# A four-layer graph network on one core: the mixes of layers 1 and 2 as three single passes, and layer 1 written in source order

## The chip, the cores and the metric

The kernel runs on one core of a Trainium2 chip. The metric is the device time of one execution in microseconds (us). The time given is the median of three runs; the profile is of one more execution, whose span and clock are given with it.

## What is computed

`x` has 32 items of 512 nodes with 128 features, in float32. `adj` is a symmetric-patterned 512 x 512 matrix, about an eighth of it nonzero. Four layers follow each other, each on `h = relu(layernorm(x))` with a residual:

```python
# layer 0: softmax over the entries of adj; own node by W[0], the others by W[1]
out = einsum('ij,bjg->big', A * M, h0) + einsum('ij,bjg->big', A * (1.0 - M), h1) + bias
# layer 1: Chebyshev hops with adj (given twice), then one projection
x1 = einsum('bnf,nw->bwf', x0, A);  x2 = 2.0 * einsum('bnf,nw->bwf', x1, A) - x0
out = relu(stack([X, x1, x2, x1, x2]) @ Theta1 + bias)
# layer 2: messages with weights = adj * adj
features = relu(h @ psi_w + psi_b)
messages = einsum('nm,bnd->bmd', weights, features)
out = relu(concat(messages, h) @ phi1_w + phi1_b) @ phi2_w + phi2_b
# layer 3: attention with a mask by adj
A = exp(8 * tanh((x @ q) @ (x @ k).T / sqrt(128) / 8)) * adj
out = (A / sum(A)) @ x @ v
```

Multiplying by the 512 x 512 matrix is called a mix here. Layer 1 has two mixes: the first makes `x1`, and since the second hop is linear, the kernel folds the five blocks of `Theta1` into three matrices `th` and mixes `h th[1] + x1 th[2]` once more, then adds `h th[0]`. Layer 2 has one mix, that of the features.

## The kernel before

The 32 items are taken as 16 pairs `q`; two pairs make a quad `r`, with `A = 2r` and `C = 2r + 1`. The 512 nodes are four tiles of 128 rows. Each item's `x` stays in SBUF from layer to layer; a transposed copy `hT` of the normalized `h` is made by stream transposes on DVE, a store of each quarter to DRAM (`d_hT`) and one load back, all issued by SP.

The mixes of layers 0, 1 and 2 are products of half blocks in the manner of Winograd: seven products of 256 x 256 blocks in place of eight, in float32. `sum_steps` (line 306) makes the sums of blocks of the matrix once, on POOL. `right_blocks` and `right_steps` (lines 343 and 350) make four differences of the right-hand side for each mix (`rt_h`, `rt_feat`, `rt_w`, line 361), on POOL and DVE. `products` (line 370) issues the seven products in the order of `ORDER`, each followed by its eviction:

```python
    ORDER = ((1, "a", True), (6, "c", True), (5, "d", True), (7, "c", False), (2, "a", False),
             (4, "c", False), (3, "d", False))
```

`by_feature` (line 381, matmul at 384) forms them for `x1T` and `msgT`, which come out transposed; `by_token` (line 387, matmul at 391) forms them for layer 0 and for the second mix of layer 1. `mixed` (line 398) evicts with two copies on ACT and six additions on DVE (lines 405 to 424); the evictions of layer 1's second mix are in `layer1` (line 964).

Layer 1 of one quad: normalize and transpose both pairs; `first` (line 978) mixes `h` into `x1T`; `straight` (line 734) copies `hT` into the order of nodes on POOL (`hs`); `weighed` (line 984) projects into `p_w` and copies that to `w` (line 987); the second mix then takes `w`, with the quad's own term `hs` by `th[0]` in the same banks. `layer2` (line 1082) projects features (`feat`, lines 1092 and 1093), mixes them into `msgT`, and applies the two phi projections.

`layer3` (line 1118) already takes its products in parts. A float32 operand is split into a high part, a low part and a middle one, each of type fp32r, and three products of the parts replace one in plain float32:

```python
    def moving_parts(x, high, low, mid):
        nc.scalar.activation(high, x, AF.Copy, scale=DOWN)
        nc.gpsimd.tensor_sub(low, x, high.bitcast(F32))
        nc.vector.scalar_tensor_tensor(mid, x, 1.0 / UP, high.bitcast(F32), OP.mult, OP.subtract)
```

These are lines 434 to 438; `scaled_parts` (line 440) does the same for the query. The scores (line 1155) go through tanh, exp (line 1160) and the mask (line 1162, on DVE and POOL in turn) into `ex`, and line 1172 multiplies `ex` with the values `hv`.

The order of the work: layer 0 stands under a manual schedule, so its instructions on PE, DVE, ACT and POOL run as the source has them. From layer 1 on the scheduler of the language orders instructions by its own estimates. What it is given is a list of generators, one for each quad of layer 1 and each pair of layers 2 and 3; the loop at line 1214 takes a new one in each turn and advances all active ones by one step, so that the steps of neighbouring quads, pairs and layers lie side by side. Buffers are rings of fixed length under a tag: `square` with four (the matrices and `ex`), `quad` with two (`w`, `msgT`, then query and values), `rt` with six, `hs` with six (also features and two parts of the keys), `u` with three (also the third part of the keys), `hT` with four. A new tile of a tag waits until the tile it replaces was last read.

Of the kernel before, what the change touches and what calls it, by code (L numbers as in the profile page):

```python
# [9 lines left out]
F32 = mybir.dt.float32  # L10
# [19 lines left out]
def kernel(  # L30
# [48 lines left out]
    work = ctx.enter_context(tc.tile_pool(name="work", bufs=4))  # L79
    bounce = ctx.enter_context(tc.tile_pool(name="bounce", bufs=4, space=bass.MemoryType.DRAM))  # L80
# [11 lines left out]
    def square_tile(name):  # L92
        return const.tile([P, NT, N], F32, tag="square", name=name, bufs=4)
# [13 lines left out]
    adj_s = square_tile("adj_s")  # L107
# [18 lines left out]
    def load_rows(ap, name):  # L126
        o = ap.shape[0] // P
        w = const.tile([P, o, ap.shape[1]], F32, name=name)
        nc.sync.dma_start(w, ap.rearrange("(o f) g -> f o g", f=P))
        return w  # L130

    def load_bcast(ap, name):
        w = const.tile([P, D], F32, name=name)
        nc.sync.dma_start(w, bass.AP(tensor=ap.tensor, offset=ap.offset, ap=[[0, P], [1, D]]))
        return w
# [6 lines left out]
    qw = load_rows(q_w, "qw")[:, 0, :]  # L142
    kw = load_rows(k_w, "kw")[:, 0, :]
# [6 lines left out]
    w0 = const.tile([P, 2, D], F32, name="w0")  # L150
    nc.sync.dma_start(w0, w_l0.rearrange("o f g -> f o g"))
    b0 = load_bcast(bias_l0, "b0")
# [27 lines left out]
    ident = const.tile([P, P], F32, name="ident")  # L180
# [6 lines left out]
    ones = const.tile([P, P], F32, name="ones")  # L187
# [118 lines left out]
    def sum_steps(mat, name, eng=nc.gpsimd):  # L306

        a11, a12 = mat[:, 0:2, 0:H], mat[:, 2:4, 0:H]
        a21, a22 = mat[:, 0:2, H:N], mat[:, 2:4, H:N]
        extra = const.tile([P, 3, 2, H], F32, tag="sums", name=f"sums_{name}", bufs=2)  # L310
        s1, s2, s4 = extra[:, 0], extra[:, 1], extra[:, 2]
        sums[name] = {1: a11, 2: a12, 3: s4, 4: a22, 5: s1, 6: s2, 7: a21}
        for out, op, p, q in ((s1, OP.add, a21, a22), (s2, OP.subtract, s1, a11),
                              (a21, OP.subtract, a11, a21), (s4, OP.subtract, a12, s2)):
            tc.keep_in_program_order(eng.tensor_tensor(out, p, q, op))
            yield

# [5 lines left out]
    def att_sums():  # L323
# [3 lines left out]
        extra = const.tile([P, 3, 2, H], F32, tag="sums", name="sums_att", bufs=2)  # L327
# [15 lines left out]
    def right_blocks(half, name, engs):  # L343

        right = {}
        for _ in right_steps(half, name, engs, right):
            pass
        return right

    def right_steps(half, name, engs, right):  # L350
        b11, b12, b21, b22 = half(0, 0), half(0, 1), half(1, 0), half(1, 1)
        if len(b11.shape) == 4:
            t = [work.tile([P, 2, 2, D], F32, tag="rt", name=f"rt_{name}_{i}", bufs=6) for i in range(4)]
        else:
            t = []
            for i in range(2):
                two = work.tile([P, 2, 2, D], F32, tag="rt", name=f"rt_{name}_{i}", bufs=6)
                t += [two[:, 0], two[:, 1]]
        right.update({1: b11, 2: b21, 3: b22, 4: t[3], 5: t[0], 6: t[1], 7: t[2]})
        for i, (p, q) in enumerate(((b12, b11), (b22, t[0]), (b22, b12), (b21, t[1]))):  # L360
            engs[i].tensor_sub(t[i], p, q)  # L361
            yield
# [18 lines left out]
    def by_feature(p, a, b, first):  # L381

        for k in range(2):
            nc.tensor.matmul(p[:, :H], b[:, k, :], a[:, k, :], start=(first and k == 0),  # L384
                             stop=(k == 1), skip_group_check=True)

# [8 lines left out]
    def u_tile(name):  # L395
        return work.tile([P, 2, H], F32, tag="u", name=f"u_{name}", bufs=3)

    def mixed(name, left, right, dst):

        m1 = dst[:, 0, H:], dst[:, 1, :H], dst[:, 1, H:]  # L400

        def evict(k, p):
            p = p[:, :H]
            if k == 1:
                nc.scalar.copy(m1[0], p)
            elif k == 6:
                nc.vector.tensor_add(m1[1], p, m1[0])
            elif k == 7:
                nc.vector.tensor_add(m1[2], p, m1[0])
            elif k == 5:  # L410
                return
            elif k == 2:
                nc.scalar.copy(dst[:, 0, :H], p)
            elif k == 4:
                nc.vector.tensor_add(dst[:, 0, H:], p, m1[0])
            elif k == 3:
                nc.vector.tensor_add(dst[:, 1, :H], p, m1[1])

        def evict2(k, p):
            evict(k, p)  # L420
            if k == 5:
                held.append(p)
            if k == 7:
                nc.vector.tensor_add(dst[:, 1, H:], held[0][:, :H], m1[2])

        held = []
        return products(name, by_feature, left, right, evict2)
# [40 lines left out]
    def quad_tile(name):  # L468
        return work.tile([P, 2, 2 * N + 2 * NT], F32, tag="quad", name=name, bufs=2)
# [8 lines left out]
    def project_steps(q, hT, copy=nc.scalar.copy):  # L478
        r, w = divmod(q, 2)
        if w == 0:  # L480
            if r % 3 == 2:
                g[r] = square_tile(f"g_{r}").rearrange("p t (b w f) -> p t b w f", b=2, w=2)
            else:
                t = quad_tile(f"g_{r}").rearrange("p w e -> p (w e)")[:, : 4 * N]
# [243 lines left out]
    late = ctx.enter_context(tc.tile_pool(name="late", bufs=4))  # L728
    for _ in range(NQ // 4, NQ // 2 - 1):
        x_tile(late, NQ // 4 - 1)  # L730
# [3 lines left out]
    def straight(hT, b, scale, name):  # L734

        s = late.tile([P, N], F32, tag="hs", name=name, bufs=6)
        src = hT[:, :, b, :].rearrange("p b (a c) -> p a b c", c=QR)
        if scale is None:
            nc.gpsimd.tensor_copy(split(s), src)
        else:  # L740
            nc.gpsimd.tensor_mul(split(s), src, split(scale))
        return s
# [7 lines left out]
    def late_sums():  # L750

        yield from sum_steps(adj_s, "adj")


        for out, op, p, q in ((1, OP.add, 1, 3), (2, OP.add, 2, 4), (0, OP.subtract, 0, 2)):
            tc.keep_in_program_order(nc.gpsimd.tensor_tensor(th[:, out, :], th[:, p, :], th[:, q, :], op))
            yield
        tc.keep_in_program_order(nc.gpsimd.tensor_scalar(th[:, 2, :], th[:, 2, :], 2.0, None, OP.mult))
# [4 lines left out]
    sums_ahead = late_sums()  # L763
# [36 lines left out]
    def round0(r):  # L800
# [4 lines left out]
        if r == 0:  # L805

            adiag.append(work.tile([P, N], F32, tag="rt", name="adiag", bufs=6))
# [148 lines left out]
    def layer0_stats():  # L956

        yield
        go(own[NQ - 2])
        go(own[NQ - 1])  # L960

    x1 = []

    def layer1(r):

        A, C = 2 * r, 2 * r + 1
        h, hT, right, hs = {}, {}, {}, {}

        def turned(q):
            hT[q] = transposed(h[q], f"hT1_{q}")  # L970
            right[q] = right_blocks(lambda J, b: h[q][:, b, 2 * J : 2 * J + 2, :], f"h_{q}", [nc.gpsimd] * 4)

        def x1T(q):
            if not x1:
                x1.append(square_tile("x1T").rearrange("p (w b) e -> p w b e", w=2))
            return x1[0][:, q % 2]

        def first(q):
            for _ in mixed(f"x1T_{q}", sums["adj"], right[q], x1T(q)):
                pass  # L980
            for b in range(2):
                hs[q, b] = straight(hT[q], b, None, f"hs_{q}_{b}")

        def weighed(q):
            for b in range(2):
                p = projected(f"p_w_{q}_{b}", (columns(hs[q, b]), th[:, 1, :]), (columns(x1T(q)[:, b]), th[:, 2, :]))
                nc.scalar.copy(w1[:, :, b, q % 2, :], p)  # L987

        h[A] = normed(A)
        yield  # L990
        turned(A)
        h[C] = normed(C)
        yield
        first(A)
        turned(C)
        yield
        w1 = quad_tile(f"w_{r}").rearrange("p w e -> p (w e)")[:, : 4 * N]
        w1 = w1.rearrange("p (t b w f) -> p t b w f", t=NT, b=2, w=2)
        weighed(A)
        first(C)  # L1000
        yield

        def operands():
            weighed(C)
            return right_blocks(lambda J, b: w1[:, 2 * J : 2 * J + 2, b], f"w_{r}",
                                [nc.vector] + [nc.gpsimd] * 3)

        sooner = r == 0 or C == NQ - 1
        if sooner:
            right2 = operands()  # L1010
        yield
        if not sooner:
            right2 = operands()
        u = [u_tile(f"l1_{r}_{i}") for i in range(3)]
        held = {}

        def own(p, I, b, first):
            straight_block(p, lambda w: hs[A + w, b], I, th[:, 0, :], first)

        def each(y):  # L1020
            return y.rearrange("p w (i f) -> p w i f", i=2)

        def finish(y, I, b):
            x = x_block(r, I, b).rearrange("p w i f -> p w (i f)")
            nc.vector.scalar_tensor_tensor(x, y, 0.0, x, OP.max, OP.add)

        def done(p, y, I, b):
# [224 lines left out]
```

## Time and profile before

| what | value |
|---|---|
| time, median of 3 runs (lowest to highest) | 946.99 us (946.71 to 947.05) |
| profiled execution, span | 946.18 us, 944.4 us |
| granted TensorE clock | 1.000 of full speed |
| busy: PE, DVE, ACT, POOL | 98%, 73%, 53%, 58% |
| layer 0, about | 0 to 184 us |
| layer 1, about | 184 to 475 us |
| layer 2, about | 446 to 678 us |
| layer 3, about | 678 to 944 us |

The profile counts an engine as busy from the start of its first to the end of its last overlapping instruction. Matmuls are pipelined, so the durations of neighbouring matmuls overlap: 1.03 us for a group of four whose next group starts 0.87 us later. A plain float32 matmul appears as two records, an fp32r one as a single record. "x4" behind a line of the timeline says how many records it stands for. A label such as `p_x1T_a<-adj_s,h` names the output and the inputs by the program's names.

### The profile page before, as it was taken

How to read it: one execution, taken by the hardware profiler on the slowest of the kernel's cores; microseconds unless marked ns; L12 is line 12 of the kernel's file. 1: busy time of each engine (PE TensorE's matmuls, PEld its weight loads, DVE VectorE, ACT ScalarE, POOL GpSimd, SP SyncE). 2: the span in 40 equal slices, each digit the busy share in tenths (PEclk: the TensorE clock that was granted, in tenths of full speed). 3: DMA queues.
4: the chain of work that ended last, by engine and by line, in shares of the span. 5: the costliest groups of instructions: out<-in, count | busy, mean ns of one | idle time of the engine just before them, and what ended most of it. 6: DMA issues, size and time to landing. Idle time of an engine off the chain costs nothing. (4 is left out here: it accounts for less than half of the span.)

```text
span 944.4 us, 15678 instructions
## 1 busy us (share of the span) xinstructions
PE 929.0 (98%) x5625; PEld 811.2 (86%) x5625; DVE 685.4 (73%) x1390; ACT 499.1 (53%) x1120; POOL 543.8 (58%) x536
## 2 busy tenths in 40 slices
PE   8999999999999999999999999999989999999997
PEld 4899999899999999899977787778779899999996
DVE  8888885745555545556667766565699999999995
ACT  5864451451241242365734855545677666666663
POOL 5878997933428524421624334433467878787873
PEclk9999999999999999999999999999999999999999
DMA  9256533242341311424333342223223121212111
GB/s 260 58 157 193 166 112 90 72 131 67 87 122 60 90 32 59 134 67 112 90 112 86 93 128 77 86 68 90 67 60 98 57 79 57 79 57 78 34 35 44
DMA packets 83916, 86.08 MB, mean 91 GB/s; under 512 B 6784, under 2 KB 74624, under 8 KB 83840
## 3 DMA queue, kind: packets, MB, share of 16 engines
q1 hardware_dynamic: 83552, 84.57, 31.8%
q8 instruction: 44, 0.72, 0.3%
q10 hardware_dynamic: 288, 0.52, 0.1%
q14 instruction: 32, 0.26, 0.1%
HBM read 44.17 MB, written 40.89 MB: 90 GB/s over the span
## 5 line engine op out<-in xcount | busy, mean ns | idle before, releaser
L252 ACT ACTIVATE h<-x,sh,rs 128x128 f32<-128x128 f32 x512 | 209.5, 485 | 46.6 <-PE p_x1T_d L384 21.6
L1172 PE MATMUL p_av<-qkh_hv,ex 128*128 128x129 f32 x1024 | 121.8, 276 | 3.2 <-POOL ex L1162 2.2
L1172 PEld LDWEIGHTS p_av<-qkh_hv,ex 128*128 128x128 f32 x1024 | 119.1, 191 | 6.2 <-POOL ex L1162 3.0
L1162 POOL TENSOR_TENSOR ex<-ex,adjTx 128x512 f32<-128x512 f32 x62 | 105.0, 1713 | 6.7 <-issue 5.7
L1162 DVE TENSOR_TENSOR ex<-ex,adjTx 128x512 f32<-128x512 f32 x66 | 87.5, 1331 | 18.4 <-ACT ex L1160 18.4
L288 DVE STREAM_TRANSPOSE hb_hT<-h 128x512 f32<-128x512 f32 x120 | 82.0, 697 | 24.2 <-ACT h L252 23.9
L232 DVE BATCH_NORM_STATS2 bn<-x 128x6 f32<-128x256 f32 x248 | 89.5, 417 | 0.5
L361 POOL TENSOR_TENSOR rt_w<-w,rt_w 128x512 f32<-128x512 f32 x16 | 20.4, 1273 | 110.3 <-DVE rt_w L361 92.0
L361 POOL TENSOR_TENSOR rt_feat<-feat,feat 128x256 f32<-128x256 f32 x16 | 11.6, 725 | 119.4 <-ACT feat L1093 119.4
L1156 ACT ACTIVATE ex<-p_score 128x512 f32<-128x512 f32 x128 | 69.7, 591 | 17.7 <-PE p_score L1155 17.6
L987 ACT COPY w<-p_w 128x512 f32<-128x512 f32 x32 | 18.2, 574 | 106.1 <-PE p_w L464 106.1
L1160 ACT ACTIVATE ex<-ex 128x512 f32<-128x512 f32 x128 | 73.2, 638 | 0.8
L437 POOL TENSOR_TENSOR key_low<-hT,key_high 128x512 fp32r<-128x512 f32 x32 | 54.5, 1702 | 32.2 <-ACT key_high L436 29.7
L444 POOL TENSOR_TENSOR query_mid<-query_high,query_low 128x512 fp32r<-128x512 f32 x32 | 41.2, 1288 | 41.5 <-PE p_qkh L1139 22.2
L442 ACT ACTIVATE query_high<-qkh_hv 128x512 fp32r<-128x512 f32 x32 | 20.2, 633 | 65.0 <-DVE qkh_hv L1142 64.2
L1155 PE MATMUL p_score<-query_high,key_high 128*128 128x512 f32 x128 | 52.4, 417 | 1.9 <-ACT query_high L442 1.9
L1155 PE MATMUL p_score<-query_mid,key_mid 128*128 128x512 f32 x128 | 50.2, 396 | 0.8 <-POOL query_mid L444 0.8
L464 PE MATMUL p_w<-th,hs 128*128 128x128 f32 x256 | 49.5, 275 | 0.0
L464 PE MATMUL p_w<-th,x1T 128*128 128x128 f32 x256 | 49.5, 275 | 0.0
L1155 PE MATMUL p_score<-query_low,key_low 128*128 128x512 f32 x128 | 49.4, 390 | 0.0
L1104 POOL TENSOR_TENSOR x<-x,phi2b 128x256 f32<-128x256 f32 x64 | 45.0, 732 | 0.0
L1093 ACT ACTIVATE feat<-feat 128x512 f32<-128x512 f32 x32 | 20.1, 629 | 41.1 <-DVE feat L1092 41.1
(256 smaller groups left out, 2373.1 us busy)
## 6 DMA issues: line engine op xcount, KB each, us to landing
d_hT<-hb_hT SPq DMA_DIRECT2D x240, 128.0 KB
hT<-d_hT SPq DMA_DIRECT2D x60, 512.0 KB
x<-in_x_dram SPq DMA_DIRECT2D x32, 256.0 KB
out_dram<-x SPq DMA_DIRECT2D x31, 256.0 KB
adjT_d<-adj_squares SPq DMA_DIRECT2D x4, 256.0 KB
sq<-in_adj_dram SPq DMA_DIRECT2D x4, 256.0 KB
adjTx<-adjT_d SPq DMA_DIRECT2D x4, 256.0 KB
adj_s<-in_adj_dram ACTq DMA_DIRECT2D x2, 256.0 KB
```

Source lines behind the costliest of these rows:

```text
L232: nc.vector.bn_stats(st[:, k].rearrange("p e s -> p (e s)"), xt[q][:, b, t : t + 2, :].rearrange("p t f -> p f t"))
L252: nc.scalar.activation(h[:, b, t, :], xt[q][:, b, t, :], AF.Relu, bias=shift[q][:, i : i + 1], scale=scale[q][:, i : i + 1])
L288: nc.vector.transpose(hb[:, :, b].rearrange("p j t r -> p t j r"), h[:, b].rearrange("p t (j c) -> p t j c", c=QR))
L437: nc.gpsimd.tensor_sub(low, x, high.bitcast(F32))
L444: nc.gpsimd.tensor_sub(mid, high.bitcast(F32), low.bitcast(F32))
L464: nc.tensor.matmul(p[:, blk(t)], hT(t), w, start=(i == 0), stop=(i == len(terms) - 1))
L1104: tc.keep_in_program_order(nc.gpsimd.tensor_add(xi, xi, spread(phi2b, 2)))
L1155: nc.tensor.matmul(ps, keys[b][i][:, t, :], query[i], start=(i == 0), stop=(i == 2))
L1156: nc.scalar.activation(ex[:, t, :], ps, AF.Tanh, scale=UP / (8.0 * math.sqrt(D)))
L1160: nc.scalar.activation(ex[:, t, :], ex[:, t, :], AF.Exp, scale=8.0)
L1162: eng.tensor_mul(split(ex[:, t, :]), split(ex[:, t, :]), crossed(adjTx[0][:, t, :]))
L1172: nc.tensor.matmul(po[:, i, : D + 1], ex[:, t, blk(i0 + i)], hv[:, t, :], start=(t == 0), stop=(t == NT - 1))
```

## The change

- `mixed_parts` takes the place of `mixed`: the right-hand side of a mix is split by `moving_parts` into high, low and mid, the matrix was split before, and 3 x 4 matmuls of 128 x 512 in fp32r go into one bank for each item; one ACT copy with a scale evicts it. `x1T` and `msgT` use it. The second mix of layer 1 does the same with the parts of `w`, which `weighed` makes straight from PSUM; its bank also takes the own term, and two DVE operations evict it into `x`. The Winograd form stays for layer 0.
- The block sums of adj and of adj squared go. `late_parts` splits adj into parts during layer 0, on ACT and POOL; `square` splits adj squared during layer 1, on POOL.
- Layer 1 is one generator under the manual schedule for PE, DVE, ACT and POOL. In each quad the second mix of the quad before stands behind the first product of this quad's pair A; the next quad's first product closes it. Two first steps of layer 2 (`more`) are written into the last quad. From there on the scheduler orders the work as before.
- The buffers move: what only layer 0 needs goes into `region0`, which is closed when layer 0 is done, and its room becomes `after`, with `wide_tile` (6 of 128 x 4 x 512: parts of `w`, of the squared matrix, `msgT`, keys, `ex`, values) and `small_tile` (13 of 128 x 512: parts of `h` and of features, `x1T`, features, the query). `matrix_tile` has three: adj, later its three parts, later the transposed mask. `hs` shares the four buffers of `hT`. The mask is loaded at the end of layer 2 instead of in layer 1.

| instructions | before | after |
|---|---|---|
| float32 records of 256 columns, layers 1 and 2 | 1344 | 0 |
| fp32r matmuls of 512 columns, layers 1 and 2 | 0 | 1152 |
| DVE, whole program | 1386 | 1314 |
| ACT | 1120 | 1192 |
| POOL | 541 | 466 |
| SP | 398 | 398 |

The core of the diff (the removal of `sum_steps`, `right_blocks`, `by_feature`, `mixed` and of the old `layer1`, and the moves of small tiles into other pools, are left out):

```diff
+    def matrix_tile(name, dtype=F32):
+        return const.tile([P, NT, N], dtype, tag="matrix", name=name, bufs=3)
+
+    def wide_tile(name, dtype=F32):
+        return after.tile([P, 4, N], dtype, tag="wide", name=name, bufs=6)
+
+    def small_tile(name, dtype=F32):
+        return after.tile([P, N], dtype, tag="small", name=name, bufs=13)
...
+    def mixed_parts(name, left, right, dst):
+
+        p = bank(f"p_{name}")
+        for part in range(3):
+            for t in range(NT):
+                nc.tensor.matmul(p, right[part][:, blk(t)], left[part][:, t, :],
+                                 start=(t == 0 and part == 0), stop=(t == NT - 1 and part == 2))
+        nc.scalar.activation(dst, p, AF.Copy, scale=UP)
...
+    def late_parts():
+
+        adj_parts.extend(matrix_tile(f"adj_{part}", F32R) for part in PARTS[:2])
+        high, low = adj_parts
+        for t in range(NT):
+            nc.scalar.activation(high[:, t, :], adj_s[:, t, :], AF.Copy, scale=DOWN)
+            tc.keep_in_program_order(nc.gpsimd.tensor_sub(adj_s[:, t, :], adj_s[:, t, :], high[:, t, :].bitcast(F32)))
+            yield
...
+        def weighed(q, b):
+            r, j = q // 2, 2 * (q % 2) + b
+            if j == 0:
+                w[r] = [wide_tile(f"w_{part}_{r}", F32R) for part in PARTS]
+            p = projected(f"p_w_{q}_{b}", (columns(hs[q][:, b]), th[:, 1, :]), (columns(x1[q, b]), th[:, 2, :]))
+            high, low, mid = (part.rearrange("p t (w f) -> p t w f", f=D)[:, :, j, :] for part in w[r])
+            nc.scalar.activation(high, p, AF.Copy, scale=DOWN)
+            nc.vector.tensor_sub(low, p, high.bitcast(F32))
+            nc.vector.scalar_tensor_tensor(mid, p, 1.0 / UP, high.bitcast(F32), OP.mult, OP.subtract)
+
+        def mix(r, i):
+            p = bank(f"p_l1_{r}_{i}")
+            for j in range(4):
+                nc.tensor.matmul(p[:, blk(j)], columns(hs[2 * r + j // 2][:, j % 2])(i), th[:, 0, :],
+                                 start=(j == 0), stop=False, skip_group_check=True)
+            for part in range(3):
+                for t in range(NT):
+                    nc.tensor.matmul(p, adj_parts[part][:, t, blk(i)], w[r][part][:, t, :],
+                                     start=False, stop=(part == 2 and t == NT - 1), skip_group_check=True)
+            nc.vector.scalar_tensor_tensor(tiles(p), tiles(p), UP, spread(b1, 4), OP.mult, OP.add)
+            x = xq[r].rearrange("p w b t f -> p (w b) t f")[:, :, i, :]
+            nc.vector.scalar_tensor_tensor(x, tiles(p), 0.0, x, OP.max, OP.add)
...
+        for r in range(NQ // 2):
...
+            else:
+                split_up(A, 1)
+                straighten(A)
+                mix(r - 1, 0)
+                normalised(C, NT)
+                turn(C, 1)
+                mix(r - 1, 1)
+                normalised(C)
+                turn(C)
+                mix(r - 1, 2)
+                split_up(C, 0)
+                go(square, r > 3)
+                mix(r - 1, 3)
+                split_up(C, 1)
+                first(A, 1)
+            weighed(A, 0)
+            weighed(A, 1)
+            go(square, r > 2)
+            first(C, 0)
+            normalised(A + 2, NT)
+            if last:
+                more(0)
+            for q in (A - 2, C - 2) if r else (NQ - 2, NQ - 1):
+                ln_stats(q) if r else go(own[q])
+            first(C, 1)
+            if r:
+                straighten(C)
+            split_up(A + 2, 0)
+            normalised(A + 2)
+            go(square, r > 3)
+            weighed(C, 0)
+            weighed(C, 1)
+            go(square, r > 3)
+            turn(A + 2)
+            first(A + 2, 0)
...
+        more(1)
+        for i in range(NT):
+            mix(r, i)
+            more(2 + i)
+        yield
...
         def key_parts(b):
-            keys[b] = [late.tile([P, NQR, P], F32R, tag="hs", name=f"key_{part}_{q}_{b}", bufs=6) for part in PARTS[:2]]
-            keys[b].append(work.tile([P, NQR, P], F32R, tag="u", name=f"key_{PARTS[2]}_{q}_{b}", bufs=3))
+            both = wide_tile(f"key_{q}_{b}", F32R)
+            keys[b] = [both[:, i].rearrange("p (t n) -> p t n", t=NQR) for i in range(3)]
             moving_parts(hT[:, :, b, :], *keys[b])
...
-            ex = square_tile(f"ex_{q}_{b}")
+            ex = wide_tile(f"ex_{q}_{b}")
```

## The prediction, made before the changed kernel ran

> **What bounds the kernel now.** First the busy shares on the page, to see which engine could set the time:
>
> ```profile
> PE 929.0 (98%) x5625; PEld 811.2 (86%) x5625; DVE 685.4 (73%) x1390; ACT 499.1 (53%) x1120; POOL 543.8 (58%) x536
> ```
>
> PE leads by 27 points. But matmul ends are modelled, so I check what PE waits for (us in total, times, longest):
>
> ```profile
> PE p_av L1172 <- POOL ex L1162: 2.2, 3, 1.0
> PE p_idle L529 <- DVE upto L194: 2.0, 1, 2.0
> PE p_score L1155 <- ACT query_high L442: 1.9, 2, 1.1
> PE p_incl L547 <- DVE rch L542: 1.0, 1, 1.0
> ```
>
> These head the list; all of it is some 15 us, no wait over 2.2. Then the windows by stage (columns: sum, then PE, PEld, DVE, ACT, POOL, clock, DMA share, GB/s): layer 0, 1, their overlap with 2, 2, 3.
>
> ```profile
> 0.00:184.00 184.00, 178.92 (x1116) 157.80 (x1117) 148.45 (x347) 98.07 (x241) 147.63 (x156) 1.00 0.50 138
> 184.00:446.00 262.00, 261.12 (x1544) 237.41 (x1543) 147.13 (x306) 96.89 (x244) 103.20 (x122) 1.00 0.32 90
> 446.00:475.00 29.00, 29.00 (x182) 26.79 (x181) 18.63 (x31) 20.88 (x52) 15.33 (x20) 1.00 0.30 74
> 475.00:678.00 203.00, 202.46 (x1024) 154.70 (x1024) 132.87 (x282) 106.20 (x248) 84.23 (x117) 1.00 0.32 91
> 678.00:944.00 266.00, 257.46 (x1766) 234.46 (x1764) 238.31 (x425) 177.07 (x337) 193.38 (x122) 1.00 0.20 62
> ```
>
> In layers 1 and 2 PE is full and no other engine passes 66%; only layer 3 has DVE near PE (90%). The clock is 1.00 throughout. What a matmul costs is read from starts in the timeline, since the durations overlap. The old mix, then the three-pass scores of layer 3, already in the form the mixes get:
>
> ```profile
> 183.55 1.03 PE L384 MATMUL p_x1T_a<-adj_s,h 128*128 128x256 f32 x4
> 184.42 1.03 PE L384 MATMUL p_x1T_c<-sums_adj,rt_h 128*128 128x256 f32 x4
> 185.28 1.03 PE L384 MATMUL p_x1T_d<-sums_adj,rt_h 128*128 128x256 f32 x4
> ```
>
> ```profile
> 802.69 0.48 PE L1155 MATMUL p_score<-query_high,key_high 128*128 128x512 f32 x1
> 803.01 0.39 PE L1155 MATMUL p_score<-query_low,key_low 128*128 128x512 f32 x1
> ...
> 805.28 0.40 PE L1155 MATMUL p_score<-query_mid,key_mid 128*128 128x512 f32 x1
> ```
>
> Four 256-column f32 records take 0.865 us: 0.216 each. Ten 512-column passes take 2.27: 0.227 each. The first pass after f32 work takes 0.32 instead: a change of form costs about 0.09.
>
> **The skill.** "FP8 and Floating Point Precision", section TensorE Precision Notes: true FP32 is four passes through the array, the reduced form one. The trace agrees: a plain 512-column f32 product shows two records of 0.430, together 3.8 times 0.227. "TensorE: Matmul & The Clock Gate", section Back-to-back issue gap: 512 columns need N/2.4 + 2.5 = 216 ns when isolated; the trace's 227 is used instead. "SBUF — State Buffer", section SBUF: two separate sides: a DVE operation with two SBUF inputs and a GpSimd operation block each other entirely; the trace agrees (query_low on DVE: 0.69 alone, up to 1.78 beside POOL).
>
> **PE, layer 1.** Per quad (four items) the two Winograd mixes have 56 + 56 records: 112 x 0.2165 = 24.2. The quad's own term is 32 records of 128 columns x 0.112 = 3.6, the p_w projection 64 x 0.112 = 7.2: 35.0. After: 48 + 48 passes x 0.228 = 21.9, six changes of form 0.5, the other two unchanged: 33.2. Saved 1.8 x 8 quads = 14.4.
>
> **PE, layer 2.** Per pair 28 x 0.2165 = 6.06 becomes 24 x 0.228 + 0.09 = 5.56; 0.50 x 16 = 8.0. Gain on PE 22.4. Bounds: 16.6 if each of the 64 changes of form costs twice 0.09, 36.2 if the 1152 passes ran at the page's 0.216. I take 22.4, since 0.227 is this trace's own rate for the same form.
>
> **The other engines' work.** Removed: 12 x 16 DVE additions of 0.42 that finish the old mixes; POOL's right-hand differences (64 rt_h and 64 rt_feat of 0.73, 24 rt_w of 1.27); the block sums. Added per 512 columns: high on ACT (0.63), low on POOL (1.27 to 1.70), mid on DVE (0.68 to 1.76) for h and features; for w, high on ACT (0.58 from PSUM) and two on DVE (0.69 each). Two PSUM evictions become one ACT copy of 0.58. Layer 1 per quad after: DVE about 24, ACT 14, POOL 10 of 33 us; layer 2 per pair DVE 8.8, ACT 9, POOL 6 of 12.6. None becomes the bound; what counts is order. In layer 0, splitting adj (8 ACT and 8 POOL steps, 5 and 10 us over five rounds, less the dropped sums) lies in POOL's idle time before its right-hand differences: 0, bounds -1 to +2.
>
> **Waits added in layer 1.** It is now written in source order on PE, DVE, ACT and POOL, so each waits for its next instruction even when a later one is ready. From the order of instructions on each engine in the changed kernel:
> - Per quad: on ACT the copy of x1T(C,1) stands behind four norms and the `sd` of two pairs. Count from W, the first projection of A. DVE finishes the last w parts at W + 2 x 1.79 + 0.8 + 2 x 0.69 = W + 5.8; then eight bn_stats of 0.42, and for the first pair `sd` on ACT, reciprocal and shift, about 2.3: the second `sd` is done at W + 11.4, and the copy ends at about W + 12.0. PE does three projections (5.4), two x1T products (2.8 each) and the hs half of the next step (0.2) first: it wants x1T(C,1) at W + 11.2. Behind the copy stand the w parts of C, hence the next mix. 0.8 x 6 quads = 4.8; bounds 0 and 12, as `sh` on DVE takes 0.16 to 1.0. In the last quad eight norms of layer 2 stand there too: 2.5.
> - Start: high of h(0,1) stands on ACT behind x1T(0,0)'s copy, which waits for PE itself: copy and splits 2.0. hs of pair 1 waits for turn(1), issued late; four stores of 0.45, landing 3.5 and the read 4.6 make 10 us, of which 2.3 shows. The late adj load on SP, ahead of d_hT1_8: 1. From quad 2 the read for A stands on SP behind a store of C; it is a quad (33 us) early: 0.
> Together 12.6, against 2.5 lost there now (261.9 elapsed for 259.4 of work at the rates above): +10.1, bounds +2 and +20.
>
> **Border of layers 1 and 2.** PE goes from the last mix to feat0 and msgT0 in turn. feat0's addition on DVE is behind mix evictions and statistics, then ACT relu and the three parts: about 5.05 after feat0 against 1.8 of PE work: 3.4 idle; the next such place 2.5; 1 elsewhere. 7 against 3.8 now (PE's 202.9 elapsed for 199.1 of work): +3.2, bounds 0 and +8. Today the scheduler interleaves the last quad with layer 2.
>
> **Layer 3.** Same arithmetic. But keys, ex and values share six wide buffers; now the keys have three places of their own, ex three and the values two. So the first tanh of ex(q,0) waits until the last score product has read the keys it replaces, and key_high for two pairs on waits for the scores of a pair before. Behind that tanh stand exp, mask (1.33 on DVE, 1.71 on POOL) and p_av. Margins before p_av are now 0.3 to 1.3 us. Bounds -2 (scheduler luck) and +16; I take +1.5.
>
> Sum: -22.4 + 10.1 + 3.2 + 1.5 = -7.6 on the 944.4 span. The profiled run took 946.18, 0.8 below the median 946.99 of the three timed ones; 946.99 - 7.6 = 939.4.
>
> **Rivals.**
> - *The forecast, a third of the gain kept*: 934 to 944. Chance 0.46.
> - *The waits are absorbed*: PE runs ahead, x1T(C,1) is in time, the border costs 1. For it: 0.8 is a small miss, and PE waits were short everywhere before. Against: four engines in order have no slack to reorder. -22.4 with 3 to 6 lost: 927.6 to 930.6. Chance 0.20.
> - *Passes gain nothing*: changes of form at the upper price leave 16.6, and waits of 15 to 19 take it: 945 to 949. Against: the score rows. Chance 0.10.
> - *Slower: layer 3's wide buffers.* DVE is at 90% there. If the late tanh eats the margin, p_av waits. It decides from 0.35 us a half step on: 32 x 0.35 = 11.2, 9.7 beyond my 1.5, puts the time at 949; at 0.75 it is 962. For it: the longest waits of today are on L1162 and L442, in this chain. Against: a whole half step of 8 us lies between reuse. With layer 1's waits at their upper bound it comes out the same. Chance 0.24.
>
> **Numbers.** Time 939.4. Range 928 to 954: leaves out the upper half of the slower rival (0.12) and the end of the absorbed case (0.04). About 1.9 us (0.2%) is what a measurement here can tell from none. Faster: 0.46, 0.20 and a little of the third: 0.69. Same 0.07, slower 0.24.
>
> **What would show it.** Starts of the passes in the mixes 0.227 apart; layer 1 per quad near 33 us plus under 1.5 of idle; in PE's waits, p_w behind x1T's copy, and p_msgT behind the parts of the first features; p_av's waits little changed. Wrong if layer 3 lasts over 270 us, if a pass in the mixes takes over 0.235, or if PE's waits in layer 1 stay under 3 us or pass 20.

## The result, and the profile after

The changed kernel takes 935.75 us (median of 4 runs, 934.17 to 939.78) against 946.85 us before (946.45 to 947.05): a ratio of 0.989, 95% interval 0.9859 to 0.9921, so 11 us or 1.1% less. The profiled execution, the fastest of the four, has a span of 932.1 us (944.4 before).

The busy line of the changed kernel, then its windows by stage (layer 0, layer 1, layer 2, layer 3; columns as before):

```profile
PE 908.0 (97%) x5433; PEld 777.9 (83%) x5433; DVE 693.7 (74%) x1318; ACT 547.6 (59%) x1192; POOL 530.3 (57%) x461
```

```profile
183.40:457.20 273.80, 268.61 (x1541) 230.75 (x1540) 163.41 (x294) 115.39 (x267) 87.11 (x84) 1.00 0.25 69
457.20:671.00 213.80, 208.19 (x1056) 159.66 (x1056) 143.29 (x262) 161.55 (x357) 105.58 (x102) 0.99 0.42 122
671.00:932.10 261.10, 251.94 (x1732) 230.22 (x1730) 240.91 (x423) 171.13 (x329) 189.29 (x123) 0.99 0.20 61
```

PE is still the engine nearest to full, and it is busy for 21 us less. But its busy time is now 5 us short of the window in layer 1 and 6 in layer 2, where it filled them before, and the clock is 0.99 in two stages. What PE waits for (us in total, times, longest) says where:

```profile
PE p_msgT L383 <- ACT high_feat L397: 4.5, 2, 2.5
PE p_av L1148 <- DVE ex L1138: 3.7, 3, 1.5
PE p_w L425 <- ACT x1T L385: 3.2, 8, 1.7
...
PE p_x1T L383 <- ACT high_h L397: 1.3, 1, 1.3
```

Of the two waits of `p_msgT`, one is at the border of layers 1 and 2 (pair 0), the other at pair 2, some 28 us later. `p_w` waits in every quad for the copy of x1T(C,1), as the prediction said: by start-to-start distances it loses 0.36 us there rather than 0.8, and 1.9 in the last quad.

Steady state, from the start of one quad's projections (one pair's second phi projection, one pair's `p_av`) to the next:

| us | before | after |
|---|---|---|
| quad of layer 1 | 35.06 | 33.65 |
| pair of layer 2 | 13.28 | 12.48 |
| pair of layer 3 | 15.88 | 15.82 |

Eight quads and sixteen pairs at these rates make 11.3 + 12.8 = 24.1 us. From the first product of layer 1 to the last of layer 2 the trace has 500.5 us before and 487.6 after, 12.9 less. So 11 of the 24 us were given back at the edges: 2.0 at the start of layer 1, 1.5 more in its last quad, 2.9 at the border, and 4.8 around the wait of pair 2 in layer 2, of which some 1.7 is not a wait at all (see the filled waits below). The first three are idle times or start-to-start distances of the changed kernel's trace, so this split is rougher than its total. Layer 3 lasts as long as before, 257.4 us for 257.0 from the last product of layer 2 to the last `p_av`.

### The profile page after: what moved, and what is told of

Same layout as the page of the kernel before. It is cut to its first block, busy times and chain, and to the rows that moved or that the text cites. A ratio compares the mean times of both kernels' runs of the same rounds, so it can differ in the third digit from the quotient of the medians.

```text
span 932.1 us, 15187 instructions
## 1 busy us (share of the span) xinstructions
PE 908.0 (97%) x5433; PEld 777.9 (83%) x5433; DVE 693.7 (74%) x1318; ACT 547.6 (59%) x1192; POOL 530.3 (57%) x461
## 4 chain that ended last, share of the span: by engine, by line
PE 87%; ACT 5%; DVE 4%; POOL 2%; issue 1%; DMA 0%; POOLq 0%; ACTq 0%; DVEq 0%
PE p_av L1148 11%; PE p_l L981 10%; PE p_msgT L383 9%; PE p_score L1131 8%; PE p_x1T L383 7%; PE p_w L425 5%; PE p_l_c L371 4%; PE p_l L977 3%; PE p_l_a L371 3%; PE p_l_d L371 3%; PE p_phi L1086 3%; PE p_phi L1087 3%; PE p_g L425 3%; PE p_l L425 3%; PE p_hv L425 3%; PE p_feat L425 3%
## 5 line engine op out<-in xcount | busy, mean ns | idle before, releaser
L1148 PE MATMUL p_av<-hv,ex 128*128 128x129 f32 x1024 | 122.7, 277 | 4.8 <-DVE ex L1138 3.7
L1148 PEld LDWEIGHTS p_av<-hv,ex 128*128 128x128 f32 x1024 | 120.3, 193 | 7.6 <-DVE ex L1138 4.5
L398 POOL TENSOR_TENSOR low_feat<-feat,high_feat 128x512 fp32r<-128x512 f32 x32 | 52.3, 1650 | 119.5 <-ACT high_feat L397 111.5
L398 POOL TENSOR_TENSOR low_h<-h,high_h 128x512 fp32r<-128x512 f32 x32 | 48.5, 1523 | 78.6 <-ACT high_h L397 78.3
L398 POOL TENSOR_TENSOR key<-hT,key 128x512 fp32r<-128x512 f32 x32 | 55.4, 1746 | 17.7 <-ACT key L397 16.9
L405 POOL TENSOR_TENSOR mid_query<-high_query,low_query 128x512 fp32r<-128x512 f32 x32 | 41.7, 1302 | 27.9 <-DVE low_query L404 14.1
L983 DVE SCALAR_TENSOR_TENSOR p_l<-p_l,b 128x512 f32<-128x512 f32 x32 | 22.4, 700 | 46.0 <-PE p_l L981 46.0
L1131 PE MATMUL p_score<-high_query,key 128*128 128x512 f32 x128 | 52.9, 417 | 0.8 <-ACT high_query L403 0.8
L1131 PE MATMUL p_score<-mid_query,key 128*128 128x512 f32 x128 | 50.3, 394 | 0.5 <-POOL mid_query L405 0.4
L1131 PE MATMUL p_score<-low_query,key 128*128 128x512 f32 x128 | 49.7, 390 | 0.0
```

The lines of the kernel that those rows point to most:

```text
L1131: nc.tensor.matmul(ps, keys[b][i][:, t, :], query[i], start=(i == 0), stop=(i == 2))
L1148: nc.tensor.matmul(po[:, i, : D + 1], ex[:, t, blk(i0 + i)], hv[:, t, :], start=(t == 0), stop=(t == NT - 1))
```

## Experiments

Unless another is named, each starts from the changed kernel, and its time stands beside 935.75. The kernel before was timed again beside each group of runs: its medians are 946.58 to 947.34 us, so under 1 us between two groups says little.

**The copy ahead of the statistics.** ACT works in order, and the copy of x1T(C,1) stands behind two `sd`, each of which waits for `bn_stats` on DVE. The timeline of ACT in the changed kernel shows it (start, us, then what was done; in brackets the idle time before it and who ended it):

```profile
402.54 0.29 ACT L249 ACTIVATE sd<-bn,eps 128x8 f32<-128x8 f32 x1
404.63 0.30 ACT L249 ACTIVATE sd<-bn,eps 128x8 f32<-128x8 f32 x1 [1.80 <-DVE bn L243]
404.85 0.58 ACT L385 ACTIVATE x1T<-p_x1T 128x512 f32<-128x512 f32 x1
405.32 0.62 ACT L397 ACTIVATE high_h<-h 128x512 fp32r<-128x512 f32 x1
```

ACT sits idle 1.80 us with the second `sd` at its head, and what PE needs comes behind it.

```diff
+            first(C, 1)
             for q in (A - 2, C - 2) if r else (NQ - 2, NQ - 1):
                 ln_stats(q) if r else go(own[q])
-            first(C, 1)
```

> Edit: in layer 1 the product x1T(C,1) and its ACT copy are written ahead of the statistics of the quad before, nothing else. Theory (the copy stands in ACT's queue behind sd, which waits for DVE): the waits of p_w for x1T in quads 0 to 6, 0.36 us each in the profile of the changed kernel, go to under 0.1; the 1.7 to 1.9 us of the last quad stays, since layer 2's norms stand there; the span falls by 2 to 2.5 us. Rival (the copy is just late by its own length, or the wait moves to the next place in the queue): p_w's waits stay near 0.36 a quad or come back as waits of p_l, span within 0.5 us.

Measured: 941.24 us (938.85 to 943.18), 5.5 slower. The waits of `p_w` for x1T are gone, but a quad takes 34.29 us instead of 33.65. (The profiled spans differ by 6.3 us: 4.7 in layer 1 between the first and the last quad, and 1.4 ahead of layer 1, where the two kernels are the same.) The first line of PE's waits names the new place:

```profile
PE p_x1T L383 <- POOL low_h L398: 5.4, 8, 0.7
```

ACT's timeline in this kernel:

```profile
408.74 0.60 ACT L385 ACTIVATE x1T<-p_x1T 128x512 f32<-128x512 f32 x1 [0.68 <-PE p_x1T L383]
409.23 0.29 ACT L249 ACTIVATE sd<-bn,eps 128x8 f32<-128x8 f32 x1
411.34 0.30 ACT L249 ACTIVATE sd<-bn,eps 128x8 f32<-128x8 f32 x1 [1.81 <-DVE bn L243]
411.55 0.61 ACT L397 ACTIVATE high_h<-h 128x512 fp32r<-128x512 f32 x1
```

The two `sd` now start later, behind the copy, and they still stand ahead of `high_h` of the next pair, hence of POOL's `low_h` and of the next quad's first product, which waits 0.68 each time. The rival was right that the wait moves to the next place in the queue; it had named `p_l` as that place and no change of the time, and neither came. That the queue behind `sd` is the mechanism is shown, here and by the next run; the remedy was wrong.

**The statistics last.** The same loop behind everything that feeds a product of this quad:

```diff
-            for q in (A - 2, C - 2) if r else (NQ - 2, NQ - 1):
-                ln_stats(q) if r else go(own[q])
             first(C, 1)
...
             weighed(C, 1)
             go(square, r > 3)
+            for q in (A - 2, C - 2) if r else (NQ - 2, NQ - 1):
+                ln_stats(q) if r else go(own[q])
```

> Edit: in layer 1 the statistics of the quad before stand behind the projections of pair C and all of their parts, ahead of the transposes. Theory (sd, which waits for DVE, blocks on ACT whatever stands behind it; here that is only the x1T copy for the next quad, which has 15 us to spare): no wait of p_w for x1T in quads 0 to 6, none of p_x1T for low_h, a quad at 33.3 us, span 2 to 2.5 us less than the changed kernel. Rival (eight bn_stats ahead of the transposes make the next pair's data late): waits of p_w for hs, or of p_l for w parts, a quad at 33.6 us or more.

Measured: every quad takes 33.16 us, the wait for x1T is gone in all eight, and the last four passes of layer 1 start at 451.76 us instead of 456.19. Yet the time is 937.06 us (936.89 to 939.55), no better. PE's timeline at the border:

```profile
451.76 1.10 PE L981 MATMUL p_l<-w_mid,adj_mid 128*128 128x512 f32 x4
454.47 2.05 PE L425 MATMUL p_feat<-psi,hT 128*128 128x128 f32 x16 [1.61 <-DMA hT<-d_hT]
461.55 2.08 PE L383 MATMUL p_msgT<-sq_high,high_feat 128*128 128x512 f32 x4 [5.02 <-ACT high_feat L397]
```

In the last quad the statistics now stand on DVE ahead of the transposes of layer 2's first pair, whose data come 1.6 us late, and the wait before `p_msgT` doubles from 2.5 to 5.0. The four passes behind it take 1.87 us instead of some 0.93: the clock fell too, to half from 460.31 on for 6.8 us. The theory held inside the layer and failed on the sum.

**Layer 2's first pair earlier.**

```diff
+            if last:
+                more(0)
             weighed(A, 0)
             weighed(A, 1)
...
+            if last:
+                more(1)
...
-        more(1)
         for i in range(NT):
+            if i == 3:
+                more(6)
             mix(r, i)
```

`more(6)` issues pair 0's features. In the final loop pair 1 is one step further and pair 2 comes in one turn sooner, so that the pairs keep their distance.

> Edit: the norms and transposes of layer 2's first pair are written before and after the projections of pair A in the last quad, and its features before the last of the four mixes of that quad; the pairs keep their distance. Theory (the border wait is the chain from features to their parts with no PE work beside it): the wait of 2.5 us before p_msgT of pair 0 goes to under 0.3, the last quad's wait of 1.7 for x1T falls under 0.5, the second wait (pair 2, 2.2 us and 0.8) stays; span 3.5 to 4.5 us less. Rival (DVE is late at the border because of mix evictions and statistics, wherever the features stand): a wait of 2 us or more stays before p_msgT of pair 0, span within 1.5 us.

Measured: 931.36 us (931.21 to 932.51), 4.4 less. The wait before pair 0's messages is gone: only pair 2's stays, 2.0 us. The last quad's wait for x1T fell to 1.1, not under 0.5.

```profile
PE p_msgT L383 <- ACT high_feat L397: 2.0, 1, 2.0
```

So the border cost what the chain features, relu, parts costs when PE has nothing beside it.

**Filled waits.** PE's timeline in the changed kernel, after the features of pair 2:

```profile
485.95 1.95 PE L425 MATMUL p_feat<-psi,hT 128*128 128x128 f32 x16
489.95 1.19 PE L383 MATMUL p_msgT<-sq_high,high_feat 128*128 128x512 f32 x4 [2.05 <-ACT high_feat L397]
491.82 2.08 PE L383 MATMUL p_msgT<-sq_low,low_feat 128*128 128x512 f32 x4 [0.67 <-POOL low_feat L398]
493.69 1.75 PE L383 MATMUL p_msgT<-sq_mid,mid_feat 128*128 128x512 f32 x4
```

The `low` passes start 0.427 us apart and not 0.227, with no wait between them. The windows around them (columns as before; the last but two is the granted clock):

```profile
488.00:491.50 3.50, 1.19 (x4) 0.67 (x4) 3.44 (x8) 2.90 (x6) 1.47 (x1) 1.00 0.00 0
491.50:495.00 3.50, 3.18 (x8) 2.52 (x9) 2.02 (x3) 1.43 (x4) 3.50 (x5) 0.53 0.78 162
```

The Trainium skill, "TensorE: Matmul & The Clock Gate", section What's actually happening, describes this: the clock falls to half after an idle window of about 3.4 us and returns after as long a busy one. To test it, products without use fill the wait:

```diff
+        if q in (0, 2):
+            filler = bank(f"p_fill_{q}")
+            for k in range(9):
+                nc.tensor.matmul(filler[:, blk(k % 4)], at(hT, 0)(k % 4), psi, start=True, stop=True)
```

> Edit: nine float32 products of 128 columns without use (about 2.0 us of PE) between the features and the messages of pairs 0 and 2, into a spare bank. The waits keep their place and their length. Theory (the passes at 0.427 us between 491 and 495 us come from the clock, which falls after idle PE time): the passes after pair 2's features run at 0.23, the granted clock there stays at 1.00, the span falls by 1.5 to 2 us, and the spread between runs gets smaller. Rival (the clock falls for another reason, or the passes are slow by a data wait): passes of 0.43 stay, span the same or 0.5 us longer.

Measured: 933.03 us (932.35 to 934.81), 2.7 less in the medians, with more work on PE and the chain no shorter. The slowest of these runs overlaps with the changed kernel's (934.17 to 939.78), and the two profiled spans are 932.9 and 932.1, so the whole time alone doesn't prove a gain. The place itself does: from the first product of pair 1's messages with phi to that of pair 2's, PE takes 17.70 us instead of 19.25. The same place in PE's timeline:

```profile
491.02 2.17 PE L1075 MATMUL p_fill<-psi,hT 128*128 128x128 f32 x18
493.24 1.20 PE L383 MATMUL p_msgT<-sq_high,high_feat 128*128 128x512 f32 x4
495.11 1.19 PE L383 MATMUL p_msgT<-sq_low,low_feat 128*128 128x512 f32 x4 [0.67 <-POOL low_feat L398]
496.14 1.07 PE L383 MATMUL p_msgT<-sq_mid,mid_feat 128*128 128x512 f32 x4
```

The `low` passes are back at 0.23 and the clock there is 1.00. The trace differs from the page in one thing: no single wait was as long as 3.4 us. Two waits of 2.05 and 0.67 with one busy stretch of 1.2 between them were enough, while a wait of 2.5 us at 459.6 us left the clock alone.

The clock records of the twelve traces, each with the moments at which the granted clock changed, say why. Apart from the one that runs on past the end of the work, every stretch at half clock lasts 3.41 us or twice that, and within a trace their starts lie whole multiples of 3.413 us apart (in the changed kernel 491.71, 689.69 and 932.03). Take this grid as a row of windows of 3.413 us each: PE, as the trace has it, was busy for a share of 0 to 0.51 of the window just ahead of each stretch. No window with a larger share was followed by the start of one, and only six with a share of 0.47 to 0.51 were not. The two waits of pair 2 lie almost whole in one window (488.30 to 491.71, share 0.35); the wait of 2.5 us is split at 460.99 (0.58 and 0.64).

So the share in a single window counts, and whether a wait of this length is followed by half clock depends on where it falls on the grid. With the products without use only 0.67 us of the wait is left, too little for any window. But the same trace has a stretch at 191.8, where the changed kernel has none, and none at 689, where that kernel has one; nothing was changed at either place. A stretch costs half its length, 1.7 us. The four runs of the changed kernel have clocks of 0.993 to 0.996, the slowest with the lowest; that difference is worth an estimated 2.8 us (0.003 of 935), half of their spread of 5.6.

**Two passes.** Is PE the bound, or is something close behind it?

```diff
-        for part in range(3):
+        for part in range(2):
```

(in both mixes, with the stop flags moved).

> Left out: the third pass (middle parts) of every mix in layers 1 and 2; the parts are still made, so all other engines keep their work. Theory (PE sets the time in both layers, with room on the others): 384 passes of 0.23 us go, 88 us less span, at least 75. Rival (DVE, with some 24 us a quad, or ACT, with 9 us a pair, is close behind, and what the next saving on PE is worth is small): 50 us less or under, with waits of p_l for w_low or w_mid, or of p_msgT for the features' parts.

Measured: 879.11 us (2 runs; 878.96 and 879.27), 57 less. A pair of layer 2 falls from 12.48 to 10.67 us, by 1.81, all of its eight passes of 0.227. A quad of layer 1 falls from 33.65 to 28.09, by 5.6 of 7.5 (32 passes): what PE waits for now is

```profile
PE p_w L425 <- ACT x1T L385: 9.3, 7, 2.7
...
PE p_w L425 <- POOL hs L952: 5.7, 7, 1.3
```

The rest went into the border, the clock (0.988) and the start of layer 3. Between the two expectations: PE bounds both layers, layer 2 with at least 14% to spare, while in layer 1 a saving of this size on PE is worth about three quarters.

**Layer 2 alone, in the kernel before.**

```diff
-        for _ in mixed(f"msgT_{q}", sums["sq"], right, msgT):
-            pass
+        for b in range(2):
+            p = bank(f"p_msgT_{q}_{b}")
+            for part in range(3):
+                for t in range(NT):
+                    nc.tensor.matmul(p, right[b][part][:, blk(t)], sq_high[0][:, t, :],
...
```

> The kernel before with the messages of layer 2 alone in three passes; layer 1 keeps its Winograd mixes and the scheduler, layer 3 its buffers. All three products take the high part of the squared matrix, whose low and middle parts are not made; the mask is loaded at the end of layer 2. Theory (a pair of layer 2 falls from 13.28 to 12.48 us because PE has less work and the waits of p_msgT for the evictions' additions go; the 8 us at the border belong to the source order of layer 1): 12.5 us a pair, 10 to 13 us less span, no wait above 1 us at the border. Rival (the gain of 0.8 a pair needs the new buffers, or half of it comes from elsewhere): 12.8 us a pair or more, 4 to 8 us less.

This kernel also lengthens the ring `rt` from six to eight buffers and loads the mask later. Measured: 946.96 us, against 946.58 of the kernel before: a ratio of 1.000 (0.9991 to 1.0009), nothing, where the theory had 10 to 13 us less and the rival 4 to 8. A pair does take 12.59 us instead of 13.28, in eleven of fifteen. But the trace has three losses that the kernel before hadn't, all in the scheduler's order: 2.8 us at the start of layer 1 with 1.7 of half clock after it; one pair of 18.97 us at the border to layer 3; about 1.7 in two pairs between. At that border, POOL's timeline and then PE's show why:

```profile
660.43 3.05 POOL L1112 TENSOR_TENSOR x<-x,phi2b 128x256 f32<-128x256 f32 x3
663.44 1.26 POOL L437 TENSOR_TENSOR low_feat<-feat,high_feat 128x512 fp32r<-128x512 f32 x1
```

```profile
664.75 2.08 PE L1106 MATMUL p_msgT<-sq_high,low_feat 128*128 128x512 f32 x4 [3.50 <-POOL low_feat L437]
```

`low_feat`, which PE waits 3.5 us for, stands behind three additions that no other engine waits for, and the clock falls after it. So the theory of the rate held, and that of the border failed: an edge between layers costs under the scheduler too.

**Layer 1 by the scheduler.**

```diff
-    next(next_layer)
-    go(made_square)
     by_source.__exit__(None, None, None)
+    next(next_layer)
+    go(made_square)
```

> The changed kernel with the manual schedule ended ahead of layer 1: the same instructions, ordered on DVE, ACT and POOL by the scheduler. Theory (source order costs 0.36 a quad plus the start and the last quad, some 7 us in layer 1, but no more): a quad at 33.3 to 33.9 us, span within 4 us of the changed kernel either way. Rival (source order is what lets the passes pay, because the scheduler puts parts and statistics ahead of copies that PE waits for): a quad above 34.5 us, span 8 us longer or more.

Measured: 941.86 us (941.26 to 943.02), 6.1 slower, between the two expectations. Six quads of seven take 33.16 us, better than the source order's 33.65 and the same as with the statistics last. One takes 40.1, and POOL's timeline shows what happened in it:

```profile
309.97 1.04 POOL L1170 TENSOR_TENSOR adj_crossed<-adj_crossed 128x512 f32<-128x512 f32 x1
310.96 1.26 POOL L1173 TENSOR_TENSOR adj_crossed<-adj_crossed,sq_high 128x512 f32<-128x512 f32 x1
312.18 1.26 POOL L398 TENSOR_TENSOR low_h<-h,high_h 128x512 fp32r<-128x512 f32 x1
```

These are the last of ten steps in a row that split adj squared, 301 to 312 us; `low_h`, needed at once, stands behind them. PE waits 5.2 us and then runs 1.6 longer at half clock. That one lump is 6.9 us, more than the whole difference. So source order isn't what makes the passes pay; its use in this trace is that `go(square, ...)` places those POOL steps where nobody waits.

**All borders together.** The statistics last, layer 2's first pair earlier, `split_up(0, 1)` ahead of `first(0, 0)`, and `next(second[2])` ahead of the final loop.

> Edits together: statistics last in a quad; the first parts of both items of pair 0 ahead of the first product of layer 1; layer 2's first pair written into the last quad, its features ahead of the last mix; pair 2 of layer 2 one step earlier. Theory (all of these are waits of in-order queues, and the clock falls only because of them): against the changed kernel 2.5 from the quads, 2 at the start, 1.5 from the last quad, 2.7 at the border, 3 and 1.8 of clock at pair 2: 11 us or so, a time of 923 to 927. Rival (part of each wait moves on to the next place): 928 to 932.

Measured: 925.59 us (924.08 to 925.97); a ratio to the kernel before of 0.9772 (0.9757 to 0.9787). All quads take 33.16. The time is 10.2 less than the changed kernel's, near the 11 expected. Of the losses, those in the quads, at the start and at pair 0 are gone or small; the one at pair 2 mostly stays, and the first three pairs of layer 2 still take 4.4 us more than three at the steady rate:

```profile
PE p_msgT L383 <- ACT high_feat L397: 1.7, 2, 1.4
```

**The operands' places.** One term of my sum was off: passes of `x1T` and `p_l` start 0.233 us apart, those of `p_msgT` 0.227. In `only_layer2` the messages took 0.233 as well; there, by the addresses of the built program, the squared matrix lay on a multiple of 64 bytes in SBUF and the other operand 32 bytes past one, as in layer 1. In layer 2 of the changed kernel both lie 32 past.

```diff
+    nc.vector.memset(const.tile([P, 8], F32, name="pad"), 0.0)
     adj_s = matrix_tile("adj_s")
```

> The version of all_borders, with an unused tile of 32 bytes a partition ahead of adj, so that the parts of adj (a multiple of 64 bytes before) start 32 bytes past one, as the parts of the squared matrix and of the right-hand sides do already. Theory (a pass takes 0.233 us in layer 1 and 0.227 in layer 2 because the two operands lie differently in SBUF): the passes of x1T and p_l fall to 0.227, 4 to 5 us less than all_borders. Rival (the rate belongs to the layer: what else runs, or the values): 0.233 stays, time within 1.5 us.

The second kernel puts that tile on the right side of SBUF instead.

> The version of all_borders, with the unused tile of 32 bytes on the other side, so that the parts of w, h, features and of the squared matrix lie on multiples of 64 bytes, as the parts of adj do. Theory (a pass is slow where its two operands lie differently): 0.227 in all mixes, 4 to 5 us less. Second theory (a pass is slow where one operand lies on a multiple of 64 bytes): 0.233 or more in all mixes, 2 us more, from layer 2. Rival (the rate belongs to the layer): 0.233 in layer 1, 0.227 in layer 2, no change.

Measured: 921.20 us (921.11 to 922.79, ratio to the kernel before 0.9735, 0.972 to 0.9749) and 922.27 us (921.11 to 922.71, ratio 0.9739). In both the low and middle passes of `p_l` fall from 0.234 to 0.2285, and a quad from 33.16 to 32.93; the passes of `x1T` stay at 0.233. Since both shifts do the same and layer 2 stays at 0.227, it isn't the multiple of 64 but the difference that goes with the rate, for `p_l`. For `x1T`, whose operands now lie alike too, the theory fails, and what holds it at 0.233 stays open; so why a difference should matter is not shown either. The quads give 1.8 of the 3 to 4 us; the rest is one stretch of half clock less in these profiles (0.998 for 0.996), which may be luck, and layer 3 at 15.79 a pair. The two are the fastest here that do all the work, and too close to each other to rank.

## Why the prediction was right, point by point

The measured 935.75 lies in the forecast's own case (934 to 944), 3.6 below its centre of 939.4. The mechanisms came as forecast: PE gains, and source order and the border give part of it back. Some terms met their number only because two errors cancelled.

- **PE, layer 1.** Predicted 33.2 us of work a quad, 1.8 less than before. Free of waits the quad takes 33.16, 1.9 less than 35.06. Two terms in it were wrong and cancel. Passes take 0.233 and not 0.228 (96 of them: +0.5). A change of form costs nothing: eight own records of 0.112 and four passes of 0.233 make 1.83, and from the own term's start at 446.02 to the `low` passes at 447.85 the trace has 1.83. I had read the first pass's 0.32 as a price; its recorded start is just early, 0.03 after the last record ahead of it (-0.5). So that the sum fits to 0.1 is luck. The lines:

```profile
446.02 1.05 PE L977 MATMUL p_l<-th,hs 128*128 128x128 f32 x8
446.83 1.19 PE L981 MATMUL p_l<-w_high,adj_high 128*128 128x512 f32 x4
447.85 1.10 PE L981 MATMUL p_l<-w_low,adj_low 128*128 128x512 f32 x4
```

- **PE, layer 2.** Predicted 0.50 a pair, measured 0.80. Without the change of form PE has 0.59 less; the other 0.21 were short waits in the old form (13.28 a pair for 13.07 of work), which I had not charged to it.
- **Waits in layer 1.** Predicted 12.6, measured 6.4: 0.36 a quad for 0.8 (in seven quads, where I had counted six), 1.9 in the last quad for 2.5, 2.0 at the start for 5.3. The mechanism was the right one; my count of DVE's steps ahead of the second `sd` was half a microsecond too long, and the loads for pair 1 didn't show.
- **Border.** Predicted 7, measured 7.7, but composed otherwise: waits of 2.9 and 3.1 and 1.7 of half clock. I had assumed that a wait costs its own length, so that the totals agree is luck.
- **Layer 3.** Predicted +1.5, measured +0.4. Six wide buffers in place of eight under three names cost nothing: 15.82 a pair for 15.88, and `p_av` waits 4.8 us in all for 3.1. The slower rival had the largest chance of the three, and the late tanh that it feared doesn't show.
- **Sum.** Layer 1 came out at -7.8 (-11.3 + 2.0 + 1.5) for the predicted -4.3, since its waits were half as long; layer 2 at -5.1 (-12.8 + 2.9 + 4.8) for -4.8, a better rate against a dearer border; layer 3 at +0.4 for +1.5. That is -12.5 for -7.6; the profiled spans differ by -12.3, the medians by -11.1. The mis-sized term that decides the difference is the waits of layer 1. "The waits are absorbed" was too hopeful by 5 us: in two of the experiments a wait that was taken away at one place came back at another.
- **Signs named beforehand.** Passes 0.227 apart: in layer 2, but 0.233 in layer 1. The waits behind x1T's copy and behind the first features' parts are there; those in layer 1 lie between 3 and 20 us, and layer 3 under 270.
- **Two slips of reading that changed nothing.** PE led DVE by 26 points (98.4% and 72.6%), not 27, and in the overlap of layers 1 and 2 ACT was busy for 72% (20.88 of 29.00 us), not at most 66.

## What to carry to other kernels

Where PE bounds a stage, count its instructions by start-to-start distance: PE's work came out within 1% here (33.2 us a quad for 33.16 free of waits, 13.07 less 0.50, or 12.57, a pair for 12.48), though in layer 1 by luck. What decides the sum is then at the edges, the first and last turn of a loop and the border of two layers, where an in-order queue has an instruction at its head that waits for another engine. Before moving such an instruction, list what will stand behind it in its new place. A wait of PE can be charged twice: once for itself and once, if PE was busy for less than about half of one window of 3.41 us, for the half clock after it. Filling such a wait with useless products took the half clock away here (1.55 us at that place); writing the next layer's first step into another took the wait itself (4.4 us of the whole time).

## What the runs showed of the hardware

- TensorE's clock was halved for 3.41 or 6.83 us at a time, on a grid of 3.413 us within each trace, and such a stretch began only after a window in which PE was busy for at most 0.51. Two waits of 2.05 and 0.67 us in one window (busy 0.35) were enough; one of 2.5 us over two windows (0.58 and 0.64) was not.
- An fp32r pass of 512 columns took 0.227 to 0.235 us. In `p_l` and `p_msgT` it was about 0.006 slower when the two operands lay 32 bytes apart in relation to a multiple of 64: a shift of either moved `p_l` from 0.234 to 0.2285. `x1T` stayed at 0.233 under both shifts.
- Going from plain float32 to fp32r products cost no time that the trace shows: eight records of 0.112 and four passes of 0.233 make 1.83 us, and 1.83 was measured.
